# Causal attention of an eight-stage network: the mask added by VectorE on the way out of PSUM, the maximum as the bias of the exponentials, their sums by ScalarE

## The chip, the cores and the metric

The kernel runs on one core of a Trainium2 chip. The metric is the device time of one execution in microseconds, as the median of several runs. An execution under the hardware profiler gives the trace.

## The reference, cut to what matters

The network passes a residual stream x of 2048 tokens (32 sequences of 64) by 256 channels through four pairs of a cross attention and a feed-forward part. The change lies in the fourth of the eight stages, the "L1 ffn": a causal attention of 16 heads of width 128 within each sequence, followed by a mixture of experts.

```
h = layernorm(x)
q, k, v = h @ wq + bq, h @ wk + bk, h @ wv + bv        # 16 heads of 128
q, k = rope(q), rope(k)                                # q * cos + rotate_half(q) * sin
scores = einsum('bhqd,bhkd->bhqk', q, k) / sqrt(128)
scores = where(causal, scores, finfo(float32).min)
probs = softmax(scores)
a = einsum('bhqk,bhkd->bhqd', probs, v) @ wo + bo
```

## The kernel before, in words

The stages A to H run one after another; D is the one that is changed, in `run_D_attention`. Tokens lie in 16 tiles of 128, each of two whole sequences. A scores tile of 128 queries by 128 keys thus holds two sequences, and its mask leaves only keys of the same sequence that are not after the query. The mask is a table of 128x128 floats, 0 or -1e30, loaded as `w["causal"]` by `load_D` (L907).

The work is cut into 64 units u. A unit is one head and one group g of four token tiles (512 tokens); block b = u // 4 stands for four heads (hg) of one group. The loop at L1153 has 72 turns, and a turn issues, in this order: `product(u-4)` (L1116), `transposed(u-3)` (L1108), `scores(u-2)` (L1090), one token tile of `output(b-2)` (L1131), `projections(u)` (L1069), one token tile of `values(b+1)` (L1059). Turns 0, 4 and 8 also take in the normalised, transposed tokens of the next group (`inputs_D`, L920, tiles in_h, hnTp and hnT). The last turns begin the routing of the experts (`routed_D`). Stage D's attention is left to the scheduler of the framework, which puts the instructions of each engine in an order of its own near this one; every engine then runs its queue in order. The mixture of experts behind it, and the large attention stages, have orders written out by hand.

What each step does on the engines:

- `projections`: ppq and ppk by PE (L1078, float32, 512 columns); VectorE adds the bias and multiplies by the cosines (L1080, rtq and rtk); ScalarE reads the same PSUM with the halves swapped (L1083, two per tile, rwq and rwk); GpSimd multiplies by the sines (L1086) and adds (L1087).
- `scores`: PE puts the mask into the PSUM tile sp by a bf16 matmul with an identity (L1093) and adds the four products of q and k (L1096). VectorE takes the maximum (L1098) and subtracts it on the way out of PSUM (L1100). ScalarE takes the exponential of the whole tile (L1101). VectorE sums (L1103), inverts (L1104) and normalises (L1105).
- `transposed`: PE transposes the probabilities (L1112, sTp), ScalarE copies them out (L1114, pT).
- `product`: probabilities times values (L1122, op), copied out with the values' bias by ScalarE (L1129, oT).
- `values`: vp (L1066), copied out by ScalarE (L1067). `output`: yp (L1137), added to the residual by VectorE (L1138).

PSUM has one buffer for sp, one for op, one for sTp and hnTp together, two for vp and yp together, three for ppq and ppk together.

Of the kernel before, what the change touches and what calls it, by code (L numbers as in the profile page):

```python
# [9 lines left out]
F32 = mybir.dt.float32  # L10
BF = mybir.dt.bfloat16
I16 = mybir.dt.int16
AF = mybir.ActivationFunctionType
ALU = mybir.AluOpType
AX = mybir.AxisListType
PSUM = bass.MemoryType.PSUM

P = 128
# [13 lines left out]
def tile_net(ctx: ExitStack, tc: tile.TileContext, a: dict, out: bass.AP):  # L32
    nc = tc.nc
    V, S, G, PE = nc.vector, nc.scalar, nc.gpsimd, nc.tensor

    def bc(ap, axis, shape):
        return ap.unsqueeze(axis).to_broadcast(shape)
# [13 lines left out]
    identb = const.tile([P, P], BF, name="identb")  # L51
# [904 lines left out]
    def run_D(w, side):  # L956
        with tc.tile_pool(name="Dh", bufs=1, side=side) as hpool:
            hs = [hpool.tile([P, D], F32, name=f"h{i}") for i in range(NT)]
            w["routed"] = {}
            w["comb0"] = hpool.tile([P, 4, 4], F32, name="comb0")  # L960

            def experts():
                w["we1"] = load(hpool, [P, 2, 4, D], a["L1_ffn_we1"].rearrange("(c p) e i -> p c e i", p=P), "we1")
                w["be1"] = load(hpool, [P, 4, 2], a["L1_ffn_be1"].rearrange("p (e c) -> p e c", c=2), "be1")
                w["be2"] = load(hpool, [4, D], a["L1_ffn_be2"].rearrange("o e d -> (o e) d"), "be2")

            w["experts"] = experts
            run_D_attention(w, side, hs)
            run_D_moe(w, side, hs)
# [54 lines left out]
    def run_D_attention(w, side, hs):  # L1024


        scale = 1.0 / float(np.sqrt(128.0))
        NU = 64
        with ExitStack() as es:
            tpool = es.enter_context(tc.tile_pool(name="Dt", bufs=1, side=side))  # L1030
            wpool = es.enter_context(tc.tile_pool(name="Dws", bufs=2, side=side))
            pool = es.enter_context(tc.tile_pool(name="Dw", bufs=2, side=side))
            psum = es.enter_context(tc.tile_pool(name="Dp", bufs=1, space=PSUM))
            hnT = [w["hnT0"]] + [tpool.tile([P, 2, 512], F32, name=f"hnT{g}") for g in range(1, NG)]
            causal = tpool.tile([P, 4, P], BF, name="causalb")
            V.tensor_copy(causal, bc(w["causal"], 1, [P, 4, P]))

            def inputs(g):
                for _ in inputs_D(w, hs, hnT[g], g, tile, psum):
# [50 lines left out]
            def scores(u):  # L1090
                qr, kr = qks.pop(u)
                sp = psum.tile([P, 4, P], F32, tag="sp", name="sp")
                PE.matmul(sp, identb, causal, start=True, stop=False, skip_group_check=True)  # L1093
                for j in range(4):
                    js = slice(j * P, (j + 1) * P)
                    PE.matmul(sp[:, j, :], qr[:, js], kr[:, js], start=False, stop=True, skip_group_check=True)  # L1096
                mx = pool.tile([P, 4], F32, name="mx")
                V.tensor_reduce(mx, sp, AX.X, ALU.max)  # L1098
                s = pool.tile([P, 4, P], F32, name="s", bufs=3)
                V.tensor_tensor(s, sp, bc(mx, 2, [P, 4, P]), ALU.subtract)  # L1100
                S.activation(s, s, AF.Exp, scale=scale)  # L1101
                sm = pool.tile([P, 4], F32, name="sm")
                V.tensor_reduce(sm, s, AX.X, ALU.add)  # L1103
                V.reciprocal(sm, sm)  # L1104
                V.tensor_tensor(s, s, bc(sm, 2, [P, 4, P]), ALU.mult)  # L1105
                ss[u] = s
# [46 lines left out]
            for u in range(NU + 8):  # L1153
                b, hh = divmod(u, 4)
                if 0 <= u - 4 < NU:
                    product(u - 4)
                if 0 <= u - 3 < NU:
                    transposed(u - 3)
                if 0 <= u - 2 < NU:
                    scores(u - 2)  # L1160
                if b >= 2:
                    output(b - 2, hh)
                if u < NU:
                    projections(u)
                    if u % 4 == 0 and b + 1 < NG:
                        inputs(b + 1)
                    if b + 1 < NU // 4:
                        values(b + 1, hh)

                if u >= NU - 3:  # L1170
                    next(ahead, None)
# [788 lines left out]
```

## Time and profile before

| | us |
|---|---|
| median of 3 runs (2780.7 to 2781.12) | 2780.76 |
| profiled execution | 2783.1 |
| its span | 2781.4 |
| PE busy | 2432.0 (87%) |
| VectorE busy | 1876.9 (67%) |
| ScalarE busy | 1531.5 (55%) |
| GpSimd busy | 1533.9 (55%) |
| mask matmul L1093, mean of 64 | 0.38 |
| maximum L1098, mean of 64 | 0.692 |
| exponential L1101, mean of 64 | 0.631 |

The profile is of one execution, and its times are counted from the start of the span. A matmul's row shows how long it was under way; matmuls overlap, so that a matmul of 0.38 us can take up much less of the chain of waits. The chain follows the work that ended last back from the end: each row is a stretch of it, with its start, its length and the engine and line. In the rows of the timeline, the bracket says how long the engine had been idle before the row, and who ended that. DVE is VectorE, ACT is ScalarE, POOL is GpSimd, PEld is PE's loading of weights.

### The profile page before, as it was taken

What the parts mean: (1) busy time and instruction counts of PE and PEld (TensorE: products, weight loads), DVE (VectorE), ACT (ScalarE), POOL (GpSimd) and SP (SyncE); (2) the same over time, 40 slices, a digit from 0 to 9 for tenths busy, and PEclk for the clock granted to TensorE, in tenths of its full rate; (3) what the DMA queues carried; (4) which work ended last, traced back from release to release, by engine and by line L of the source; (5) the groups of instructions that cost most, each with busy time, mean ns of one, the idle gap of its engine ahead of it and who ended that gap; (6) DMA issues with size and microseconds to landing.
All of it is one profiled execution on the core that took longest, in us unless ns stands there. A gap on an engine that the chain in (4) does not pass through costs nothing.

```text
span 2781.4 us, 44370 instructions
## 1 busy us (share of the span) xinstructions
PE 2432.0 (87%) x16078; PEld 1432.5 (52%) x16078; DVE 1876.9 (67%) x3919; ACT 1531.5 (55%) x2181; POOL 1533.9 (55%) x1764
## 2 busy tenths in 40 slices
PE   4999899778778778779999999979898887789999
PEld 2545344344444444446666666756555543456565
DVE  7888554899999999965454545666577758833232
ACT  1666321699999999846555555524255457831111
POOL 4665543588888888765555555503488765720000
PEclk9999999999999999989999999989999998989999
DMA  6553000699999999920000000001343412000000
GB/s 167 133 123 75 23 1 1 142 197 209 199 205 203 198 207 205 198 82 1 16 8 24 8 1 1 16 31 51 76 97 88 96 35 67 1 0 8 8 8 8
DMA packets 610599, 223.70 MB, mean 80 GB/s; under 512 B 547366, under 2 KB 600524, under 8 KB 605772
## 3 DMA queue, kind: packets, MB, share of 16 engines
q1 hardware_dynamic: 607308, 220.07, 36.1%
q8 instruction: 127, 2.08, 0.3%
q10 hardware_dynamic: 3072, 0.79, 0.2%
q14 instruction: 92, 0.75, 0.1%
HBM read 66.91 MB, written 18.87 MB: 31 GB/s over the span
## 4 chain that ended last, share of the span: by engine, by line
PE 47%; DVE 20%; issue 9%; POOL 5%; ACT 2%; DMA 1%; ACTq 0%; SPq 0%; POOLq 0%; DVEq 0%
DVE e L840 11%; PE yp L1137 4%; PE ppq L1078 4%; PE ppk L1078 4%; PE pgate L1836 4%; PE pup L1836 3%; PE hout L1812 3%; PE vp L1066 3%; PE sp L1096 2%; PE op L1122 2%; POOL e L291 2%; PE ep L1207 2%; PE hmp L1194 2%; PE sc L812 1%; PE op L801 1%
## 5 line engine op out<-in xcount | busy, mean ns | idle before, releaser
L864 ACT ACTIVATE ei<-e,nb,sq 128x2048 int16<-128x2048 f32 x256 | 535.4, 2092 | 39.7 <-DVE nb L861 36.2
L874 POOL CAST eb<-ei 128x2048 bf16<-128x2048 int16 x256 | 481.9, 1892 | 110.8 <-ACT ei L864 93.6
L812 PE MATMUL sc<-kT,qz 128*128 128x512 bf16 x1024 | 296.8, 380 | 142.0 <-DVE e L840 140.0
L251 DVE TENSOR_REDUCE negm<-s 128x2 f32<-128x512 f32 (+1 forms) x512 | 301.1, 611 | 125.7 <-PE s L247 122.4
L840 DVE TENSOR_SCALAR_CACHE_REDUCE e<-sc,mx 128x1024 f32<-128x1024 f32 x256 | 326.1, 1274 | 0.4 <-DVE nb L861 0.3
L840 DVE TENSOR_SCALAR_CACHE_REDUCE e<-sc 128x1024 f32<-128x1024 f32 x256 | 312.5, 1221 | 4.8 <-PE sc L812 4.8
L283 ACT ACTIVATE e<-s 128x1024 f32<-128x1024 f32 (+1 forms) x256 | 233.0, 915 | 148.7 <-PE s L279 110.6
L812 PEld LDWEIGHTS <-qz 128*128 128x128 bf16 x1024 | 94.5, 97 | 260.2 <-issue 202.6
L247 PE MATMUL s<-stk,stq 96*128 96x256 bf16 (+1 forms) x1024 | 191.6, 270 | 40.8 <-DMA d3k<-t3k 24.5
L1086 POOL TENSOR_TENSOR rwq<-rwq,sin 128x512 f32<-128x512 f32 x64 | 81.1, 1268 | 239.3 <-ACT rwq L1083 225.0
L279 PE MATMUL s<-stq,stk 128*128 128x256 bf16 (+1 forms) x1024 | 179.6, 261 | 8.7 <-DMA stq<-nm 5.0
L825 PEld LDWEIGHTS <-vz 128*64 128x64 bf16 x4096 | 123.3, 110 | 112.7 <-issue 112.3
L1846 DVE TENSOR_TENSOR hm<-pup,sl 128x512 f32<-128x512 f32 (+1 forms) x56 | 38.7, 691 | 200.5 <-PE pup L1836 193.6
L1098 DVE TENSOR_REDUCE mx<-sp 128x4 f32<-128x512 f32 x64 | 44.3, 692 | 190.6 <-PE sp L1096 190.6
L1083 ACT ACTIVATE rwq<-ppq,dbq 64x512 f32<-64x512 f32 x128 | 87.3, 682 | 153.7 <-DVE rtq L1080 150.2
L825 PE MATMUL av<-eT,vz 128*64 128x128 bf16 x4096 | 163.9, 223 | 5.9 <-DMA eT<-eb 5.8
L247 PEld LDWEIGHTS <-stq 96*128 96x128 bf16 x1024 | 93.5, 100 | 130.3 <-issue 107.5
L301 PE MATMUL o<-e,vmo 128*32 128x256 f32 (+1 forms) x2048 | 150.2, 365 | 7.2 <-POOL e L291 5.8
L291 POOL TENSOR_SCALAR_AFFINE_SELECT e<-e 128x256 f32<-128x256 f32 (+1 forms) x256 | 132.7, 545 | 31.2 <-ACT e L283 31.1
L1844 ACT ACTIVATE sl<-pgate 128x512 f32<-128x512 f32 (+1 forms) x56 | 33.4, 597 | 207.8 <-PE pgate L1836 207.8
L1066 PE MATMUL vp<-Dwv,hnT 128*128 128x512 f32 x256 | 122.1, 599 | 6.0 <-ACT hnT L945 5.5
L91 POOL TENSOR_TENSOR rstd<-ve,mhalf 128x1 f32<-128x1 f32 (+1 forms) x40 | 25.8, 646 | 182.8 <-DVE mv L424 69.2
(404 smaller groups left out, 5468.3 us busy)
## 6 DMA issues: line engine op xcount, KB each, us to landing
stk<-d3k SPq DMA_DIRECT2D x96, 192.0 KB
stq<-d3q SPq DMA_DIRECT2D x96, 192.0 KB
d3k<-t3k SPq DMA_DIRECT2D x160, 64.0 KB
d3q<-t3q SPq DMA_DIRECT2D x96, 64.0 KB
eT<-eb SPq DMA_TRANSPOSE x256
fw<-in_L_ffn_w SPq DMA_DIRECT2D x3, 1024.0 KB
x<-in_x SPq DMA_DIRECT2D x16, 128.0 KB
c<-in_ctx SPq DMA_DIRECT2D x16, 128.0 KB
```

The costliest lines, as they stand in the source:

```text
L247: PE.matmul(sc[:, hh, lo:hi], qs[0:96, 2 * hp + hh, qc * P : (qc + 1) * P], ks[0:96, 2 * hp + hh, lo:hi], start=band is None, stop=True, s ...
L251: V.tensor_reduce(negm[:, qc, 2 * hp : 2 * hp + 2], sc[:, :, lo:hi], AX.X, ALU.max, negate=True)
L283: S.activation(e[:, :, lo:hi], sc[:, :, lo:hi], AF.Exp, scale=scale)
L291: G.affine_select(e[:, :, s0:s1], e[:, :, s0:s1], [[0, 4], [step, s1 - s0]], ALU.is_ge, 0.0, base=base, channel_multiplier=chan,)
L812: PE.matmul(sc[:, k0 : k0 + 512], qz[i % 2][:, h, :], kT[:, h // 2, 1024 * part + k0 : 1024 * part + k0 + 512], start=True, stop=True,)
L825: PE.matmul(av[i][r0 : r0 + 64, h // 4, :], vz[:, kt, h // 4, h % 4, :], eT[:, kt, :], start=h == 0 and kt < 2, stop=h == H - 1 and kt >= ...
L840: V.tensor_scalar(e, scs.pop((n, part)), 1.0, mx[:, 0:1] if part else LOWEST, ALU.mult, ALU.max, accum_out=mx[:, part : part + 1],)
L864: S.activation(ei, es_.pop(n), AF.Exp, bias=nb, scale=sq[i][:, h : h + 1], accum_out=sums[i][:, h : h + 1],)
L874: G.tensor_copy(eb, eis.pop(n - 1))
L1066: PE.matmul(vp, hnT[g][:, c, j * P : (j + 1) * P], wv[:, c, :], start=c == 0, stop=c == 1)
L1078: PE.matmul(pp, wt[:, c, hh * P : (hh + 1) * P], hnT[g][:, c, :], start=c == 0, stop=c == 1)
L1836: PE.matmul(pp[:m], w[nm + "s"][:, c, cols], xnT[:, c, :], start=c == 0, stop=c == 1)
```

## The change

The mask's matmul goes, and with it the bf16 copy of the mask, which had been cast once at the start of the stage. The four score products each write their part of sp afresh. VectorE adds the float32 mask as it brings sp into SBUF; it takes the maximum from there, and multiplies it by minus the scale. ScalarE takes the exponential in four instructions of 128 columns, one per token tile, since each has its own bias (the maximum) per query; each also gives the sum of its row. VectorE's sum goes.

```
-            causal = tpool.tile([P, 4, P], BF, name="causalb")
-            V.tensor_copy(causal, bc(w["causal"], 1, [P, 4, P]))
...
                 sp = psum.tile([P, 4, P], F32, tag="sp", name="sp")
-                PE.matmul(sp, identb, causal, start=True, stop=False, skip_group_check=True)
                 for j in range(4):
                     js = slice(j * P, (j + 1) * P)
-                    PE.matmul(sp[:, j, :], qr[:, js], kr[:, js], start=False, stop=True, skip_group_check=True)
+                    PE.matmul(sp[:, j, :], qr[:, js], kr[:, js], start=True, stop=True)
+                s = pool.tile([P, 4, P], F32, name="s", bufs=3)
+                V.tensor_tensor(s, sp, bc(w["causal"], 1, [P, 4, P]), ALU.add)
                 mx = pool.tile([P, 4], F32, name="mx")
-                V.tensor_reduce(mx, sp, AX.X, ALU.max)
-                s = pool.tile([P, 4, P], F32, name="s", bufs=3)
-                V.tensor_tensor(s, sp, bc(mx, 2, [P, 4, P]), ALU.subtract)
-                S.activation(s, s, AF.Exp, scale=scale)
+                V.tensor_reduce(mx, s, AX.X, ALU.max)
+                V.tensor_scalar(mx, mx, -scale, None, ALU.mult)
                 sm = pool.tile([P, 4], F32, name="sm")
-                V.tensor_reduce(sm, s, AX.X, ALU.add)
+                for j in range(4):
+                    S.activation(
+                        s[:, j, :], s[:, j, :], AF.Exp, bias=mx[:, j : j + 1], scale=scale, accum_out=sm[:, j : j + 1]
+                    )
                 V.reciprocal(sm, sm)
                 V.tensor_tensor(s, s, bc(sm, 2, [P, 4, P]), ALU.mult)
```

In the changed kernel the order of the instructions on GpSimd and on the DMA queues is the same as before. On VectorE and ScalarE it is the same but for the replaced instructions, and for turns 4, 5, 8 and 9 and the last turns, where the new instructions, the copies of hnT, pT and oT, and the in_h steps change places. On PE the scores, transposes and products change places in those turns too.

## The prediction, written before the result was known

> **What bounds the kernel now.** I read the busy time by stretches first, to find the stage of the change and the engine that is full there; the instructions of its lines (L1066 to L1138) lie between 1196 and 1816 us. Columns: stretch, length, busy us of PE, its weight loads, VectorE, ScalarE and GpSimd, then the granted clock.
>
> ```profile
> 1300.00:1400.00 100.00, 100.00 (x446) 66.83 (x445) 50.04 (x85) 54.45 (x87) 54.44 (x44) 1.00 0.04 11
> 1500.00:1600.00 100.00, 100.00 (x440) 66.57 (x439) 51.45 (x88) 52.87 (x86) 53.63 (x43) 1.00 0.03 9
> ```
>
> TensorE is busy throughout at full clock, the others are near half. A busy PE need not be the bound, so next the chain of waits, over one turn of the loop:
>
> ```profile
> 1434.76 0.44 PE sTp L1112 x4
> 1435.19 0.21 PE sp L1093
> 1435.41 0.89 PE sp L1096 x8
> 1436.30 1.73 PE yp L1137 x8
> 1438.03 1.72 PE ppq L1078 x4
> 1439.75 1.72 PE ppk L1078 x4
> 1441.46 1.72 PE vp L1066 x4
> 1443.18 0.89 PE op L1122 x8
> 1444.07 0.44 PE sTp L1112 x4
> ```
>
> Only PE stands in it, without a gap. A turn is 9.31 us (1434.76 to 1444.07), and the mask's matmul, L1093, is 0.215 of it (0.21 and 0.22 in turns). Third, the timeline of the same turn, to see how far the softmax is from delaying PE:
>
> ```profile
> 1436.34 0.69 DVE L1098 TENSOR_REDUCE mx<-sp 128x4 f32<-128x512 f32 x1 [3.33 <-PE sp L1096]
> 1437.06 0.69 DVE L1100 TENSOR_TENSOR s<-sp,mx 128x512 f32<-128x512 f32 x1
> 1437.79 0.63 ACT L1101 ACTIVATE s<-s 128x512 f32<-128x512 f32 x1 [1.61 <-DVE s L1100]
> 1439.38 0.69 DVE L1105 TENSOR_TENSOR s<-s,sm 128x512 f32<-128x512 f32 x1
> ```
>
> Scores end at 1436.30, probabilities at 1440.07: 3.77 us. PE transposes them at 1444.07, 7.77 us after the scores (yp 1.73, three projections 5.16, op 0.89). So 4.0 us are free.
>
> **The change, part by part.**
>
> *The mask's matmul and weight load go (64 times)*, each 0.215 us of the path. Number 0 saves nothing: it ran at 1220.97, while PE was about to wait for the rotated keys until 1221.64. Nor does number 63: PE then waited 0.28 us for rtk L1087. Number 1 ran on the half clock, 0.43. That is 62 x 0.215 + 0.43 = 13.8; I take 13.5, since PE has short idle times around the input turns. Could the mask be hiding the first weight load of the scores? At the end of the stage the chain has scores straight after transposes:
>
> ```profile
> 1798.90 0.44 PE sTp L1112 x4
> 1799.34 0.22 PE sp L1096 x2
> ```
>
> 0.11 us each, as inside a run of scores (0.89 / 8). I book nothing. If a load of 0.135 us (eight in 1.08 at L1096) came out each time, 62 x 0.135 = 8.4 us would go; a gain here is excluded.
>
> *The cast L1036 goes*: 0.43 us of VectorE at 1181.2, where VectorE had been waiting for PE's av and nobody waited for it. Nothing.
>
> *VectorE's steps.* The addition reads PSUM and writes SBUF, like L1100: 0.69. The maximum now reads SBUF, like L1103: 0.69. The 128x4 multiplication: 0.18, as the reciprocal L1104. The sum L1103 (0.69) goes. VectorE has 0.5 us less per turn, off the path. The new multiplication may be held up, though, because it falls while GpSimd still rotates the next keys (until 1438.19, 1.9 us after the scores):
>
> ```profile
> 1223.86 1.27 POOL L1087 TENSOR_TENSOR rtq<-rtq,rwq 128x512 f32<-128x512 f32 x1
> 1224.04 1.11 DVE L932 SCALAR_TENSOR_TENSOR in_stats<-in_stats 128x4 f32<-128x4 f32 x1
> ```
>
> The 128x4 step, elsewhere 0.16, ended with GpSimd's. The Trainium skill, "GPSIMD Engine Reference", section 1, "Specifications", says that VectorE instructions in a two-port mode or with two SBUF inputs contend with GpSimd. By its words the addition (one input in PSUM) is free, the normalisation L1105 is not (one L1105 does take 1.73 against a median of 0.69), and the multiplication only if it gets the two-port mode; L931, a one-input 128x4 step, took 0.50 once instead of 0.17, so I think it does. Between 0 and one GpSimd step, 1.27; I take 0.6.
>
> *ScalarE: four exponentials with bias and sum for one of 0.63.* No row has this form. Nearest is the summing 128x256 activation with its read of the sum:
>
> ```profile
> 2338.49 0.43 ACT L1624 ACTIVATE gjunk<-c 128x256 f32<-128x256 f32 x1
> 2338.80 0.21 ACT L1624 ACTIVATION_READ_ACCUMULATOR gjunk<-c 128x1 f32 x1
> 2338.90 1.09 ACT L1501 ACTIVATE xq<-xk,rndup,sca 128x256 f32<-128x256 f32 x2
> ```
>
> The next instruction starts 0.41 after it. Half the columns take off about 0.1 (128x256 copies from PSUM 0.37, 128x128 0.27), a bias tile puts about 0.1 on (128x512: copy 0.59, L1129 with bias 0.69): 0.41 each, 1.7 for four with the last read. The Trainium skill, "ScalarE: Activation LUTs", section "What ACT_TABLE_LOAD costs", gives about 280 ns + 0.833 ns per column with a bias pointer, so 0.39, with 0.19 for the read (L864's row) 0.57: an estimate of 2.3 for four with nothing overlapped. This rule speaks against the change: the fixed cost is paid four times for the same columns. The row, which shows the overlap, sets the value, 1.7; 1.4 and 2.6 are the ends. ScalarE goes from 5.0 to 6.1 us per turn of 9.1: still not the bound. Exp was there before among Identity and Copy without a table load in this stage; none is added.
>
> *The new chain of a turn*: 0.69 + 0.69 + 0.18 + 0.6 + 1.7 + 0.18 + 0.69 and 0.25 of gaps = 5.0 against 3.77, still 2.8 us before PE wants it. The reciprocal now waits for ScalarE where the sum did; behind it on VectorE stand the normalisation, rtq and rtk of the projections. Behind those on ScalarE are rwq, rwk, v, oT and pT, on GpSimd the rotation. rtq comes 1.2 later, but rtk already waits 0.83 for ppk, so it moves about 0.4. GpSimd's rotated keys were ready 6.1 us before their scores (1438.19 to 1444.34); a later chain of 1.2 leaves 4.9. In the steady turns nothing reaches PE.
>
> *Where the cover is missing.* (a) The first transposes: PE waited 5.56 us for s until 1233.52. The maximum had started at 1229.58; now 0.69 + 0.69, the multiplication behind GpSimd's step until 1231.46, exponentials 1.7, 0.2 + 0.75: ready near 1234.4 instead of 1233.37. Costs 1.0. (b) Turn 4 (1244.15 to 1252.60, end of scores to end of scores) takes in a group of inputs: ScalarE has 5.0 + 8 hnT pieces at a pitch of 0.40 = 8.2 of 8.45 us. With 1.1 more it is fuller than PE, and the new order of instructions puts the four exponentials between the third and last pair of hnT, which PE's transposes share a PSUM bank with. Excess 9.3 - 8.24 = 1.1; I take 1.0. (c) Turn 8 (10.6 us) has room, but its order is similar: 0.7. (d) The last turns: the chain in front of rtq of unit 63 is 1.2 later and PE was already waiting for rtk: 1.2. Sum 3.9, between 0 and 9.0 (with one more GpSimd step of 1.27 at each of the four).
>
> **Sum.** 13.5 - 3.9 = 9.6 us. Profiled execution 2783.1 (span 2781.4 and 1.7 around it): 2773.5. The median of the runs is 2.3 under that execution, 2780.76: 2771.2.
>
> **The rivals.**
>
> *Nothing is lost at the turns with inputs*: 2780.8 - 13.5 = 2767.3. For it: PE is hardly idle after 1234 before. Against it: the full ScalarE in turn 4. 12%.
>
> *A weight load comes out behind the transposes*: 13.5 - 8.4 - 3.9 = 1.2 saved, 2779.6. Against it stands the row at 1799.34. 8%.
>
> *The losses at start, inputs and end eat most of it* (about 9 of 13.5): 2776.3. For it: in-order queues with GpSimd's steps in between, and the changed order around turns 4 and 8. 10%.
>
> *Slower: ScalarE's four exponentials take the path.* Place: between the multiplication and the reciprocal of every turn. All else of the chain is 2.7 to 3.9 us, so PE starts to wait once a quarter costs over (7.77 - 3.3) / 4 = 1.1 us. At 1.4 each turn is 1.2 longer, less 0.215: 60 x 1.0 = 60 us, 2840; slower than before from about 1.2 each. The nearest row (0.41 pitch, 0.57 by the rule) is far from it. 4%.
>
> **How the numbers follow.** Main case 66%: 2771.2, itself 2768 to 2775. Measurement of this kernel tells 0.2% (5.6 us) from no change: under 2775.2 is faster. Main and first rival give 0.78, a third of the losses case 0.03: 0.81 faster. Two thirds of that case and the exposed load give 0.15 within, 0.04 slower. The range 2767 to 2777.5 leaves out the exposed load, the slow case and the edges.
>
> **What would show it.** Right: the chain at 1400 to 1700 is PE alone, with sp L1093 (its new line) straight after sTp, a turn of 9.10 us and the stage at full PE. The exponentials' rows show 0.4 to 0.45 us and the reads 0.19, at a pitch near 0.41; the new multiplication's maximum is far above its minimum. PE's waits for s at the first transposes grow to some 6.6 us. Wrong: gaps of PE in the steady turns (at sTp by s, or at sp by rtk), a first score piece over 0.11 in the chain, or a stage that is shorter by the full 13.8.

## The result, and the profile after

The changed kernel takes 2770.55 us (median of 6 runs, 2769.68 to 2776.34) against 2780.94 (6 runs) before: a ratio of 0.9966, with a 95% interval of 0.9953 to 0.9979. It is faster by about 10 us; 2771.2 had been forecast. The profiled execution took 2769.79 us, with a span of 2768.1.

The busy time by stretches in the profile after (columns as before):

```profile
1300.00:1400.00 100.00, 100.00 (x441) 66.15 (x441) 51.12 (x90) 66.59 (x166) 54.62 (x45) 1.00 0.04 11
1500.00:1600.00 100.00, 100.00 (x441) 66.26 (x440) 50.28 (x88) 66.13 (x165) 55.39 (x45) 1.00 0.02 6
```

PE is still busy all the time. ScalarE has gone from 53 to 54 us in a hundred to 66, and VectorE has stayed near 51. One turn in the chain of waits. In the kernel after, the lines from the scores on have other numbers (the scores' products are L1093, ppq and ppk L1076, vp L1064):

```profile
1432.99 0.44 PE sTp L1112 x4
1433.43 0.89 PE sp L1093 x8
1434.32 1.73 PE yp L1137 x8
1436.05 1.72 PE ppq L1076 x4
1437.77 1.72 PE ppk L1076 x4
1439.48 1.72 PE vp L1064 x4
1441.20 0.89 PE op L1122 x8
1442.09 0.44 PE sTp L1112 x4
```

The mask's row is gone, the scores follow the transposes at the same 0.89 us, and a turn is 9.10 (1432.99 to 1442.09). Next, the softmax of the following turn in the timeline; its scores end at 1443.42 in the chain.

```profile
1443.46 0.69 DVE L1095 TENSOR_TENSOR s<-sp,causal 128x512 f32<-128x512 f32 x1 [3.06 <-PE sp L1093]
1443.90 1.26 POOL L1084 TENSOR_TENSOR rwk<-rwk,sin 128x512 f32<-128x512 f32 x1
1444.19 0.69 DVE L1097 TENSOR_REDUCE mx<-s 128x4 f32<-128x512 f32 x1
1444.91 0.29 DVE L1098 TENSOR_SCALAR mx<-mx 128x4 f32<-128x4 f32 x1
...
1445.29 0.40 ACT L1101 ACTIVATE s<-s,mx 128x128 f32<-128x128 f32 x1 [0.97 <-DVE mx L1098]
1445.60 0.19 ACT L1101 ACTIVATION_READ_ACCUMULATOR s<-s,mx 128x1 f32 x1
1445.69 0.39 ACT L1101 ACTIVATE s<-s,mx 128x128 f32<-128x128 f32 x1
...
1447.18 0.69 DVE L1105 TENSOR_TENSOR s<-s,sm 128x512 f32<-128x512 f32 x1
```

The probabilities are ready at 1447.87, 4.45 us after the scores, where it was 3.77. The four exponentials with their reads follow each other every 0.39 to 0.40 us, 1.65 together. PE wants the probabilities 7.77 us after the scores, so 3.3 us are still free in this turn.

To find where the rest went I divided the stage at marks on PE: the first vp, the first transposes (T), the ends of the scores of units 2, 4, 6, 8 and 60 (counted from 0), and the first matmul of the experts. The segments "scores 2, 4" and "scores 6, 8" hold the turns 4 and 8, which take in inputs. All in us, from the starts and ends in the trace. The last column books 0.215 us for each mask that leaves (0.43 for the one on the half clock); only in the steady turns is it measured.

| from, to | before | after | difference | of it, masks gone |
|---|---|---|---|---|
| vp, T | 37.44 | 38.18 | +0.74 | 0 |
| T, scores 2 | 10.63 | 11.46 | +0.83 | -0.64 |
| scores 2, 4 | 16.70 | 17.86 | +1.16 | -0.43 |
| scores 4, 6 | 15.17 | 14.75 | -0.42 | -0.42 |
| scores 6, 8 | 20.58 | 21.21 | +0.63 | -0.43 |
| scores 8, 60 | 480.86 | 469.77 | -11.09 | -11.09 |
| scores 60, experts | 38.85 | 39.92 | +1.07 | -0.43 |
| stage | 620.23 | 613.15 | -7.08 | -13.44 |

So the stage is 7.1 us shorter: 13.4 booked as saved, 6.4 lost at start, inputs and end. The two spans differ by 13.3; the other 6.2 us lie outside the stage.

### The profile page after: what moved, and what is told of

It is laid out like the page before. It is cut to its first block, busy times and chain, and to the rows that moved or that the text cites. A ratio compares the mean times of both kernels' runs of the same rounds, so it can differ in the third digit from the quotient of the medians.

```text
span 2768.1 us, 44646 instructions
## 1 busy us (share of the span) xinstructions
PE 2397.4 (87%) x15910; PEld 1418.7 (51%) x16014; DVE 1865.1 (67%) x3918; ACT 1598.3 (58%) x2629; POOL 1534.3 (55%) x1764
## 4 chain that ended last, share of the span: by engine, by line
PE 46%; DVE 20%; issue 9%; POOL 5%; ACT 3%; DMA 1%; ACTq 0%; POOLq 0%; DVEq 0%
DVE e L840 11%; PE yp L1137 4%; PE ppq L1076 4%; PE ppk L1076 4%; PE hout L1812 3%; PE pgate L1836 3%; PE pup L1836 3%; PE vp L1064 3%; POOL e L291 2%; PE op L1122 2%; PE sp L1093 2%; PE ep L1207 2%; PE hmp L1194 2%; PE sc L812 1%; PE op L801 1%
## 5 line engine op out<-in xcount | busy, mean ns | idle before, releaser
L812 PE MATMUL sc<-kT,qz 128*128 128x512 bf16 x930 | 280.7, 380 | 155.8 <-DVE e L840 151.9
L1095 DVE TENSOR_TENSOR s<-sp,causal 128x512 f32<-128x512 f32 x64 | 44.3, 692 | 165.7 <-PE sp L1093 165.7
L1101 ACT ACTIVATE s<-s,mx 128x128 f32<-128x128 f32 x256 | 99.6, 390 | 80.5 <-DVE mx L1098 80.5
L1064 PE MATMUL vp<-Dwv,hnT 128*128 128x512 f32 x256 | 122.2, 599 | 7.6 <-ACT hnT L945 7.1
```

Of the source, the lines that this page charges most:

```text
L812: PE.matmul(sc[:, k0 : k0 + 512], qz[i % 2][:, h, :], kT[:, h // 2, 1024 * part + k0 : 1024 * part + k0 + 512], start=True, stop=True,)
L1064: PE.matmul(vp, hnT[g][:, c, j * P : (j + 1) * P], wv[:, c, :], start=c == 0, stop=c == 1)
```

## The experiments

The stage's length is measured in each as in the table. "The rest" is the span less the stage. A single execution's total time is not compared, since the rest scatters by as much as the stage changes.

**The two kernels once more, unchanged.**

> The kernel before, profiled once more. The stage is measured from its first matmul of the values (vp) to the first matmul of the experts (hmp): 620.2 us before, 613.1 after, so 7.1 of the profiles' difference of 13.3. Theory: the stage repeats within 0.3 us, and the other 6.2 us are scatter of the other stages, so the rest of the program comes out anywhere within some 5 us of the first profile (2161.2 before, 2155.0 after). Rival: the change shortens the other stages too; then the rest repeats at 2161.

Measured: stage 620.29, rest 2161.1, every segment within 0.04 us of the first profile.

> The changed kernel, profiled once more. Theory: the stage repeats 613.1 us, within 1.6 us since the half-clock stretch behind the first transposes has come out between 3.0 and 6.1 us in the profiles so far; the rest of the program, 2155.0 in the first profile of it and 2158.9 to 2164.1 in the four others whose other stages are the same, comes out inside or near that band, 2158 to 2164. Rival (the change shortens the rest): 2155 again.

Measured: stage 613.4, rest 2159.3. So the stage repeats, also in the half-clock stretch, and the rest of the changed kernel does not stay at 2155.0. Over the other kernels below, whose other stages are the same, it is 2156.4 to 2167.0. The stages ahead of the changed one scatter alike: the first vp starts between 1194.0 and 1202.7 us in the 14 profiles (1196.1 and 1196.5 before; 1194.4, 1194.3 and 1200.0 after). So I take the 6.2 us of the first pair of profiles as scatter.

> The changed kernel in five more rounds. Theory (the gain is the stage's, 620.2 - 613.2 = 7.0 us, and the rest of the program only scatters): ratio to before near 0.9975. Rival (the gain is the 10.4 us between the medians of the first runs): 0.9963.

Measured: 2773.58 us, ratio 0.9953 with an interval of 0.9939 to 0.9967; stage 613.7, rest 2161.7. Here the kernel before had 2786.01 (9 runs, 2780.86 to 2788.66). The ratio is nearer to the rival's, and the 7.0 us of the stage (0.9975) lie outside this interval, though inside the first one. At least 2 us of the gain in these runs are thus not accounted for by the stage. In the rest the profiles have 2161.2 and 2161.1 before and 2155.0, 2159.3 and 2161.7 after: a mean 2.5 us lower after, but with a scatter of 6.7 us in three profiles. So whether the change also shortens the rest stays open.

**The mask left out.** Only the mask's matmul and the cast go; the softmax is the old one, and the causal mask is missing from the computation. The edit is against the kernel before.

```
-            causal = tpool.tile([P, 4, P], BF, name="causalb")
-            V.tensor_copy(causal, bc(w["causal"], 1, [P, 4, P]))
...
-                PE.matmul(sp, identb, causal, start=True, stop=False, skip_group_check=True)
...
-                    PE.matmul(sp[:, j, :], qr[:, js], kr[:, js], start=False, stop=True, skip_group_check=True)
+                    PE.matmul(sp[:, j, :], qr[:, js], kr[:, js], start=True, stop=True)
```

> The kernel before without the mask's matmul and without any mask (the causal mask is left out of the computation), softmax as before. Theory: PE's place in the turn is all that the mask cost, and nothing is lost elsewhere as the softmax chain is the old one: the stage is 620.2 - 13.5 = 606.7 us, turns of 9.10. Rival (the mask's time is partly hidden, or a weight load comes out): 610 to 615.

Measured: 609.7. The turns are 9.10 and the segments with inputs shrink by the masks alone (16.27, 20.15), as my theory had it. The 3.0 us by which it missed stand in two places. The half clock behind the first transposes lasted longer (11.78 instead of 10.63 in that segment; why is told below), and at the end the masks' time didn't come out (39.49 against 38.85). The chain of waits shows what sets the end instead:

```profile
1790.57 1.27 POOL rwk L1084
...
1791.93 1.28 POOL rtk L1085
...
1793.25 1.16 PE sp L1093 x8
```

The last scores wait for GpSimd's last rotated keys, however early PE is.

**The exponentials alone.** The mask stays with PE; multiplication, four exponentials straight from PSUM, and sums by ScalarE. The edit is against the kernel before.

```
                 V.tensor_reduce(mx, sp, AX.X, ALU.max)
...
-                V.tensor_tensor(s, sp, bc(mx, 2, [P, 4, P]), ALU.subtract)
-                S.activation(s, s, AF.Exp, scale=scale)
+                V.tensor_scalar(mx, mx, -scale, None, ALU.mult)
...
-                V.tensor_reduce(sm, s, AX.X, ALU.add)
+                for j in range(4):
+                    S.activation(
+                        s[:, j, :], sp[:, j, :], AF.Exp, bias=mx[:, j : j + 1], scale=scale, accum_out=sm[:, j : j + 1]
+                    )
```

> The mask stays PE's; only the second part of the change: maximum times -scale, four exponentials with bias straight from PSUM, sums by ScalarE. Theory: steady turns stay at 9.31, the stage pays only at the start, in turns 4 and 8 and at the end, 2 to 6 us: 622 to 626. Rival (the longer chain costs a little in every turn): 60 turns by 0.1 or more, so over 628.

Measured: 623.8. Steady turns are unchanged (480.86 for 52). It loses 0.7 up to the first transposes, 1.4 behind them (half clock), 1.0 in turn 4, 0.6 in turn 8, and nothing at the end (38.84). This part of the change is a loss by itself, at three of the four places that were named.

**The mask alone.** VectorE adds the mask; the softmax is the old one, its subtraction now from SBUF to SBUF. The edit is against the changed kernel, as are all that follow.

```
-                V.tensor_scalar(mx, mx, -scale, None, ALU.mult)
+                V.tensor_tensor(s, s, bc(mx, 2, [P, 4, P]), ALU.subtract)
+                S.activation(s, s, AF.Exp, scale=scale)
...
-                for j in range(4):
-                    S.activation(
-                        s[:, j, :], s[:, j, :], AF.Exp, bias=mx[:, j : j + 1], scale=scale, accum_out=sm[:, j : j + 1]
-                    )
+                V.tensor_reduce(sm, s, AX.X, ALU.add)
```

> Mask by VectorE as in the changed kernel, but the softmax of before (subtraction as its own step, one exponential, sum by VectorE). The chain is 0.7 us longer than before, all on VectorE, ScalarE's load as before. Theory: turns of 9.10; the start loses 0.7 us and up to 1.3 by the half clock, turns 4 and 8 about 1 together instead of 2.6: stage 609 to 611. Rival (any longer chain costs the same, whichever engine holds it): 613 as in the changed kernel.

Measured: 610.4, inside the expected range, but not for my reason. Turn 8 loses only 0.1 (20.27), yet the segment of turn 4 is 17.60, nearly as in the changed kernel, with ScalarE's old load. The chain has this there:

```profile
1250.59 0.70 DVE mx L1097
...
1251.31 1.70 DVE s L1098
1253.01 0.67 DVE rtq L1078
```

The subtraction, a step of 0.7 us, took 1.70: now that it reads SBUF it is held up as the small multiplication is (in 41 of 64 units it takes more than 1 us). This kernel differs in one thing more that had not been expected: the scheduler puts VectorE's next step on the projections ahead of the normalisation (rtk at the first transposes, rtq in the last turns). The start loses 1.5 us (38.93), and the end is 0.8 shorter than before (38.06).

**The multiplication gone.** The scale moves into the masking step, and the maximum comes out negated, which gives the bias without a step of its own.

```
-                V.tensor_tensor(s, sp, bc(w["causal"], 1, [P, 4, P]), ALU.add)
+                V.scalar_tensor_tensor(s, sp, scale, bc(w["causal"], 1, [P, 4, P]), ALU.mult, ALU.add)
-                V.tensor_reduce(mx, s, AX.X, ALU.max)
-                V.tensor_scalar(mx, mx, -scale, None, ALU.mult)
+                V.tensor_reduce(mx, s, AX.X, ALU.max, negate=True)
...
-                        s[:, j, :], s[:, j, :], AF.Exp, bias=mx[:, j : j + 1], scale=scale, accum_out=sm[:, j : j + 1]
+                        s[:, j, :], s[:, j, :], AF.Exp, bias=mx[:, j : j + 1], scale=1.0, accum_out=sm[:, j : j + 1]
```

> The changed kernel without the 128x4 multiplication: the scale goes into the step that adds the mask, and the maximum comes out negated. Theory: the multiplication took 0.59 in the median (0.16 to 1.28, held up by GpSimd), so the chain is 0.4 to 0.8 us shorter: nothing in the steady turns, 0.3 to 0.8 at each of start, turns 4 and 8 and end; stage 611 to 612 at an equal half-clock stretch. Rival (the hold-up moves on to the next step): 613.

Measured: 608.4, 4.7 us less than the changed kernel; I had expected 1 to 2. The masking step costs what it did:

```profile
1448.38 0.69 DVE L1095 SCALAR_TENSOR_TENSOR s<-sp,causal 128x512 f32<-128x512 f32 x1 [3.12 <-PE sp L1093]
1449.11 0.69 DVE L1097 TENSOR_REDUCE mx<-s 128x4 f32<-128x512 f32 x1
```

The segments are 37.68, 10.32, 16.63, 14.75, 20.23, 469.78 and 39.02: 0.5 less up to the first transposes, 1.1 behind them, 1.2 and 1.0 in the turns with inputs, and 0.9 at the end. With ScalarE's load as in the changed kernel, turns 4 and 8 lose only 0.4 and 0.1 against the kernel without a mask. The order that the scheduler chose around turn 4 is another too (two of the exponentials now come behind the last hnT), so in turn 4 the shorter chain and the order are not told apart.

> Scale in the masking step and negated maximum, without the 128x4 multiplication, timed: the stage was 608.4 us in one profile, 11.8 under before. Theory: ratio near 0.9958. Rival (the 4.7 us against the changed kernel were a lucky phase of that execution): stage 611 to 613 in this profile and 0.9970 or more.

Measured: 2771.4 us, ratio 0.9948 (0.9936 to 0.9961), stage 608.3. The stage's gain is not a chance of one execution.

**PE kept busy in front of the first transposes**, in the changed kernel, by 24 matmuls that nobody reads.

```
+            w["sinb"] = tpool.tile([P, 512], BF, name="sinb")
+            V.tensor_copy(w["sinb"], w["sin"])
...
+                if u == 0:
+                    fill = psum.tile([P, 512], F32, tag="op", name="fill")
+                    for _ in range(24):
+                        PE.matmul(fill, identb, w["sinb"], start=True, stop=True)
```

> The changed kernel with 24 bf16 matmuls of identity and sines into an unused PSUM tile (their result is never read) in front of the first transposes, where PE idled 6.3 us. Theory: that idle time brings the half clock, so with PE busy the first transposes, scores and ppq run at full speed: 0.65 + 0.82 + 1.30 = 2.8 us less, stage 610.3. Rival (the slow stretch is a matter of the operands or of PSUM): stage 613.

Measured: 611.3. The segment behind the first transposes goes from 11.46 to 8.90, so the idle time was what brought the half clock. But turn 4 gives 0.5 back (18.37): the multiplication behind the scores of unit 2 is held up there for 0.94 us, where it was 0.45 in the changed kernel.

The same matmuls in the kernel without the multiplication:

> The same with the 24 matmuls that keep PE busy in front of the first transposes (the result is not read). Theory: the half-clock stretch goes, 1.4 us against the last kernel's 10.3 us segment from first transposes to third scores, less 0.5 that turn 4 gave back in the other kernel with them: stage 607 to 607.5, ratio 0.995 to 0.9955. Rival (turn 4 gives all of it back): 608.4.

Measured: 2769.96 us, ratio 0.9939 (0.9927 to 0.9952), stage 607.0; the segment is 8.90 and turn 4 gives nothing back (16.63). It has the lowest median here, but its interval overlaps that of the kernel without these matmuls (0.9936 to 0.9961), so only the stage's 1.3 us tell the two apart.

**ScalarE's time in the chain raised**, by extra exponentials in front of the four.

```
+            junk = tpool.tile([P, P], F32, name="junk")
...
+                for j in range(4):
+                    S.activation(
+                        junk, s[:, j % 4, :], AF.Exp, bias=mx[:, j % 4 : j % 4 + 1], scale=scale,
+                        accum_out=sm[:, j % 4 : j % 4 + 1],
+                    )
```

> The changed kernel with four more exponentials of the same form in front of the four (written to a tile that nobody reads; the sums are then overwritten): ScalarE's step of the chain grows by 4 x 0.39 = 1.55 us. Theory: 2.8 us of the steady chain were free, so turns stay at 9.10 with PE alone in the chain of waits, and only start, turns 4 and 8 and the end lose, 1 to 1.6 each: stage 617 to 620. Rival (ScalarE's time is felt in every turn): 52 turns by 0.2 or more, over 624.

Measured: 621.6. The busy time by stretches:

```profile
1500.00:1600.00 100.00, 100.00 (x441) 66.19 (x440) 50.99 (x88) 84.02 (x253) 54.96 (x45) 1.00 0.02 6
```

ScalarE is at 84, and PE does the same 441 matmuls in the hundred us. In the steady turns 1.55 us on ScalarE cost nothing; the loss of 8.5 us is at start, inputs and end, a little more than expected (at the end a stretch of half clock, 6.83 us from 1797.83, comes in too).

> The changed kernel with twelve more exponentials of 128 columns in front of the four (not read, sums overwritten), 12 x 0.39 = 4.7 us more on ScalarE per turn. This is the slow rival of the prediction brought about: the chain from scores to probabilities becomes 4.4 + 4.7 = 9.1 us against the 7.77 that PE leaves, and ScalarE has 6.0 + 4.7 = 10.7 us of work per turn against PE's 9.10. Theory: turns of 10.7 to 11, ScalarE full, stage 613 + 52 x 1.7 = 700 or more. Rival (PE stays the bound, as with four more): 625 to 632.

Twelve instead of four, otherwise the same edit. Measured: stage 789.9. The same row:

```profile
1500.00:1600.00 100.00, 86.35 (x343) 51.52 (x341) 36.58 (x71) 97.45 (x342) 43.53 (x35) 0.97 0.05 16
```

ScalarE is full and PE has fallen to 343 matmuls. A turn is 11.7 us (608.7 for the 52 turns from the scores of unit 8 to those of unit 60). That is more than expected because ScalarE has more to do: 97% of 11.7 is 11.4 us a turn, against the 10.7 that had been reckoned. The scheduler weaves the extra exponentials in among ScalarE's other steps, and where two of them follow each other they start 0.53 us apart and not 0.39. So the slow rival exists, but well beyond what four exponentials cost.

## Why the prediction was right, point by point

**Time and sign.** Right: 2771.2 forecast, 2770.55 measured. But the stage gave 7.1 us and not 9.6, which alone would have made 2773.7. The medians differ by 10.4, so some 3 us of the gain lie outside the stage, where nothing had been forecast: that the number came out so near is in part luck.

**What bounds it, and what the mask's matmul is worth.** Right. PE alone stands in the chain of the steady turns before and after, a turn goes from 9.31 to 9.10, and the 52 steady turns give 11.1 us, 0.213 for each mask where 0.215 had been taken. That no weight load comes out is shown by the 0.89 us of the scores behind the transposes.

**The exponentials.** Right: 0.39 each and 0.19 for the read, 1.65 for four where 1.7 had been taken from the row of the summing activation. The 2.3 that the page's figures gave with nothing overlapped was too high: in the timeline each read starts some 0.1 us before its exponential ends, and the next exponential 0.1 us before the read ends.

**The multiplication.** Right in kind. All 64 in the profile after (least, median and greatest ns):

```profile
L1098 DVE TENSOR_SCALAR mx<-mx x64: 155/592/1281, 1229.3 to 1791.9; 128x4 f32<-128x4 f32 x64
```

In 49 of the 64 it took more than 0.25 us, and each of these ended 0.02 to 0.03 us after the GpSimd step that was under way when it began. The addition, one of whose inputs is in PSUM, was never held up (0.68 to 0.69), as the prediction had read the page. (The one-input step L931 that it shows as held up once was so twice, 0.56 and 0.50 us.) 0.78 in all had been taken, and the median is 0.59. (In the turn shown it took 0.29, and the whole chain 4.45 where 5.0 had been reckoned.) In the steady turns it costs nothing. In the others it costs more than was booked, as the kernel without it shows.

**The losses, 3.9 forecast, 6.4 measured.** The loss comes out about midway between the main case and the rival that put it at 9. Here the terms were mis-sized, one was missing, and in two the cause was wrong or not enough:

- The start: 1.0 forecast, 0.74 measured.
- Behind the first transposes nothing was booked beyond the masks, and 1.47 went. The stretches around them, before and after (stretch, length, busy us of PE, granted clock, share and GB/s of the DMA):

```profile
1232.85:1236.26 3.41, 2.74 (x12) 0.50 0.02 5
1236.26:1239.67 3.41, 3.41 (x11) 1.00 0.00 0
```

```profile
1231.00:1234.41 3.41, 1.86 (x9) 0.50 0.00 0
1234.41:1237.82 3.41, 3.41 (x9) 0.50 0.02 5
1237.82:1241.24 3.42, 3.42 (x10) 1.00 0.00 0
```

  The clock is halved for 3.41 us before and for twice that after. In the chain, first before, then after, ppq comes out at 3.02 us instead of 1.72:

```profile
1233.52 1.09 PE sTp L1112 x4
1234.60 0.43 PE sp L1093
1235.03 1.54 PE sp L1096 x8
1236.57 1.72 PE ppq L1078 x4
```

```profile
1232.55 1.09 PE sTp L1112 x4
1233.63 1.71 PE sp L1093 x8
1235.34 3.02 PE ppq L1076 x4
```

  Transposes and scores were at half speed before, too; the second stretch is new. The transposes had come 0.67 us after the clock was halved, and now come 1.55 us after it. The last section shows that over ten profiles the later ones go with the second stretch. This is the term that the prediction lacked: it delayed the transposes by 1.0 us and left the half clock as long as it was.
- Turn 4: 1.0 forecast, 1.59 measured; turn 8: 0.7 and 1.06. What PE waits for in turn 4, first the row before, then two after:

```profile
1248.69 1.13 PE L1066 MATMUL vp<-Dwv,hnT 128*128 128x512 f32 x2 [0.21 <-ACT hnT L945]
```

```profile
1249.62 1.12 PE L1064 MATMUL vp<-Dwv,hnT 128*128 128x512 f32 x2 [0.62 <-ACT hnT L945]
1259.83 1.16 PE L1122 MATMUL op<-pT,v 128*128 128x128 f32 x8 [0.76 <-ACT pT L1114]
```

  In turn 8 it is the first hnT alone, 1.54 us for 0.41 before. That hnT stands on ScalarE behind the exponentials and two rwq, so a longer chain delays it; pT stands in the new order behind two rwq and one rwk. So the place was right, but the reason given, ScalarE fuller than PE, is not enough: with the same load on ScalarE but without the multiplication the turns lose 0.4 and 0.1 (PE waits 0.36 for hnT, and not for pT), and with ScalarE's old load but a subtraction that GpSimd can hold up, turn 4 loses 1.3. The wait at the PSUM bank that hnT shares with the transposes is 0.10 us.
- The end: 1.2 forecast, 1.50 measured, and again for another reason. The kernel without a mask, whose chain is not longer, loses 1.07 there, and the one with four exponentials but PE's mask loses nothing. The end waits for GpSimd's last keys, which come at a pace of their own: those of unit 63 start 7.95 to 7.97 us after those of unit 62, before, after, without a mask and with the exponentials alone, while PE's own turn there is 7.60 or 7.38. GpSimd's step holds up the normalisation (1.72 us before and 1.43 after, instead of 0.69), rtq stands behind that on VectorE, rwq and rwk behind rtq on ScalarE, and GpSimd's next step behind those. Where VectorE takes rtq ahead of the normalisation, in the kernel with the mask alone, the pace is 6.59 and the end is shorter. So the masks in the last turns don't count; two of them had been counted as saved.

**The rivals.** The slow one was rightly set aside: four extra exponentials leave the steady turns alone, twelve put them on ScalarE. The point from which it decides was put at a step of some 4.4 us in the chain, against 1.65 measured; the experiments bracket it between 3.2 and 6.3 (estimates: 1.65 and four or twelve times 0.39 more).

## What to carry to other kernels

When one engine's work alone makes up the chain of waits, a step taken off it pays in full in every steady turn, and what the other engines do for it is free up to the slack, which is read from the timeline as the time between "ready" and "wanted". The losses are in the turns that aren't steady: start, refills and end. There a small step in the middle of a chain can cost more than its work, so look for a form that does without it, such as a scale folded into a step that is there anyway and a maximum that comes out negated. Read the granted clock behind each long wait of PE: a wait that grows by 1 us can bring a second stretch of half clock. And look in the last turns for a ring of other engines that is slower than PE: what PE saves there is not gained.

## What the runs showed of the hardware

VectorE steps that read and write SBUF can be held up by a GpSimd step under way: the 128x4 multiplication took 0.16 to 1.28 us, and a 128x512 subtraction up to 1.80 (median 1.20) once it read SBUF, where it had taken 0.69 from PSUM. The maximum, which reads SBUF and writes only four columns, never was (0.674 to 0.690 in all 64).

After PE has been idle for 5.6 to 7.0 us in front of the first transposes, the granted clock is 0.50 for 3.41 or for 6.83 us, nothing in between. With the idle time filled it stays at 1.00 there. Which of the two it is goes with how far into the half clock the transposes come:

| profiles | transposes after the clock is halved, us | half clock, us |
|---|---|---|
| before (two) | 0.67, 0.72 | 3.41 |
| without the multiplication (two) | 0.45, 0.72 | 3.41 |
| without a mask | 0.92 | 6.83 |
| exponentials alone | 1.29 | 6.83 |
| changed (three) | 1.55, 1.45, 1.30 | 6.83 |
| mask alone | 3.10 | 6.83 |

So the kernel without a mask had the second stretch too, and the one without the multiplication had not. This is what ten profiles have in common; no run moved the transposes alone, and what decides between 0.72 and 0.92 was not tested.

A read of ScalarE's sum costs little in a row of summing exponentials: with it, the next one starts 0.39 us after the one before, which is the duration of the exponential alone. Twelve extra ones that all write the same tile start 0.53 us apart where two of them follow each other; why was not tested.
